# Weight loads on ScalarE's queue, and the last sums an eighth later, in a local-attention and whitening kernel

## The chip, the cores and the metric

The kernel runs on one core of a Trainium2 chip. A core has a matrix engine (TensorE, PE in the profile), a vector engine (VectorE, DVE), a scalar engine (ScalarE, ACT), a general engine (GpSimd, POOL) and SyncE (SP), which here only issues transfers. Each has its own queue of instructions and takes them in order; they meet through semaphores. PEld is the loading of weights into the matrix engine. The metric is device microseconds of one execution; the lower, the better.

## The reference

The input x has four images of 256 channels and 64 x 64 pixels, in float32.

```
k    = conv(x, w1, 7x7, dilation 2, pad 6) + b1      # 256 -> 128
k    = conv(k, w2, 1x1) + b2                         # 128 -> 49
attn = softmax(k, axis=1)                            # 49 taps for each pixel
xp   = pad(x, 6)
x    = sum over u, v of attn[7u + v] * xp[.., 2u:2u+64, 2v:2v+64]

# whitening, for each of four groups of 64 channels, over all images and pixels
xc    = x - mean;  Sigma = 1e-5 * I + xc @ xc.T / m
Sn    = Sigma / trace(Sigma);  P = I
5 times:  P = 1.5 * P - 0.5 * P^3 @ Sn
out   = (P / sqrt(trace(Sigma))) @ xc * weight + bias
```

So each image needs a convolution before its weighted sum, and the whitening matrix needs the sums of all four images before any output can be written.

## The kernel before

The two convolutions are one, with 49 outputs (w2 times w1). It is evaluated in seven points for each axis: the input of each of seven row points (`conv_step`) is combined on VectorE (`xh`, `ct`), multiplied on TensorE, and interpolated back on VectorE (`pv`, `zz`, at last `lgx`, the logits). A row point has three banks of column points, with one set of weights (`wr`) each. For the first image the transformed weights are made on the chip and written to DRAM (`gd`); for the later images `weights` loads them again (L419: 42 loads of about half a megabyte, in one buffer for each bank number). `conv_bank` does the matmuls of a bank (L599) into one of two PSUM buffers, `cv_buf`, and ScalarE copies them out (`pv`, L610 and L615).

The weighted sum of an image is cut into four units, n = 4b to 4b + 3, by parity of rows and columns, and each unit into `first_half` and `second_half`. `softmax(b, pc)` prepares two units: TensorE transposes the logits (L990), VectorE takes their maximum (L996), ScalarE the exponential, VectorE normalises and shuffles (L1034). `move_terms(n)` copies the terms into `zt` (L1075 on ScalarE; for the last image L1087 on VectorE), GpSimd writes them to DRAM (`sd`, L1092, eight transfers), and `load_band` reads them back skewed, as band matrices (L1127 and L1138, on SyncE). `make_block` transposes the pixels (L1168) and copies them to `xb` and `xbz` (L1174, L1182); `weighted_sum` multiplies them with the bands (L1210); `store_y` brings the result to SBUF (L1228, L1230); `turn_y` transposes it again (L1241, copied by ScalarE at L1249), and `moments` adds to mean and covariance (L1262). Transposes share three PSUM buffers, which `tp()` hands out. `make_block` and half of `store_y` use VectorE instead of ScalarE once `tail` is set. After odd units `move` may write a finished part of an image to DRAM (`spill`, L1280, 2 MB on GpSimd) and load other pixels in its place.

Two things set the order. The first is an order written by hand: the loop over images 1 to 3 takes the convolution's steps with costs of 6, 5 and 2, and each time an eighth of an image's cost is done, `gap(b, j)` runs what `plan` has put down for that eighth: the softmax of the image before, then its eight half-units. What is planned beyond the last eighth of image 3 runs after the convolution, with `tail` set. The second is the planner of the kernel language, which within this gives every engine its order by data and priorities. `softmax(b, 0)` and the copies under `high_priority` go first. `whiten` and the loop that applies it and writes the output follow, when all units are summed.

For the last two images the half-units stand at eighths 3 to 10 of the next image, in the kernel before: for image 3 all of them, and for image 2 the last three, lie after the convolution.

Of the kernel before, what the change touches and what calls it, by code (L numbers as in the profile page):

```python
# [32 lines left out]
def kernel(  # L33
# [29 lines left out]
    nc = tc.nc  # L63
    B, C, H, W = x.shape
# [30 lines left out]
    def taps(b):  # L95
        return (0,) if b == INF else (0, 1)
# [12 lines left out]
    def tp():  # L109
        return ps_tp.tile([P, 512], F32, tag="tp", name="tp")  # L110
# [72 lines left out]
    t = tp()  # L183
# [3 lines left out]
    t = tp()  # L187
# [4 lines left out]
    cv_buf = []  # L192
    for k in range(2):
        t = ps_cv.tile([P, 512], F32, name=f"cv{k}")
# [53 lines left out]
    for k, c0 in enumerate(range(0, P, CB)):  # L248
        n = min(CB, P - c0)
        t = cv_buf[k % 2]  # L250
# [15 lines left out]
    for k0 in range(0, KT, TB):  # L266
        n = min(TB, KT - k0)
        t = tp()
# [44 lines left out]
    for b in ORDER:  # L313
        slot_of[b] = nsl
        nsl += len(taps(b))
    gd = [
        dram.tile([P, nsl, NSK * len(taps(b)) // 2], F32, name=f"gd{b}") for b in range(NP)
    ]
# [27 lines left out]
    def add(o, a, b):  # L346
        return in_turn(TT(o, a, b, ALU.add))  # L347
# [57 lines left out]
    def weights(b, br, i, mid=None):  # L405

        first = (br, i) not in made
        made.add((br, i))
        s0 = slot_of[BANKS[i][0]]
        ns = sum(len(taps(bc)) for bc in BANKS[i])
        nk = NSK * len(taps(br)) // 2
        wt = apool.tile([P, ns, NSK], F32, tag=f"wr{i}", name=f"wr_{b}_{br}_{i}")[:, :, :nk]
        w = {bc: wt[:, slot_of[bc] - s0 : slot_of[bc] - s0 + len(taps(bc))] for bc in BANKS[i]}
        if not first:
            nc.sync.dma_start(wt, gd[br][:, s0 : s0 + ns])  # L419
            return w  # L420

        if br in kept:


            f = lgx if br == 4 else rb[0].rearrange("p q r c w -> p (q r c w)")
            f = f[:, : KS * nk]
            if i == 0:
                nc.sync.dma_start(f, kept[br])
            f = f.rearrange("p (v a r k) -> p v a r k", v=KS, a=NCC, k=KT)
            g = [f[:, v] for v in range(KS)]  # L430
        else:
            g = [gbr[:, v] for v in range(KS)]
        g = [t.rearrange("p a r k -> p (a r k)") for t in g]

        e = ct.rearrange("p a b -> p (a b)") if b else store[4].rearrange("p c r w -> p (c r w)")
        e, o, e1 = (e[:, k * nk : (k + 1) * nk] for k in range(3))
        g0 = [g[KS - 1 - a] for a in range(4)]
        g1 = [g[KS - 5 - a] for a in range(3)]
        o0 = {bc: w[bc][:, 0] for bc in w}
        o1 = {bc: w[bc][:, 1] for bc in w if bc != INF}  # L440

        def same(o, a):
            if br in kept:
                v = KS - 1 - a
                nc.sync.dma_start(o, kept[br][:, v * nk : (v + 1) * nk])
            else:
                nc.scalar.copy(o, g[KS - 1 - a])

        if i == 0:
            add(e, g0[0], g0[2])  # L450
            add(o, g0[1], g0[3])
            add(e1, g1[0], g1[2])
            add(o0[1], e, o)
            sub(o0[2], e, o)
            add(o1[1], e1, g1[1])
            sub(o1[2], e1, g1[1])
            same(o0[0], 0)
            same(o1[0], 4)
        elif i == 1:
            madd(e, g0[2], 4.0, g0[0])  # L460
            madd(o, g0[3], 4.0, g0[1])
            madd(e1, g1[2], 4.0, g1[0])
            madd(o0[3], o, 2.0, e)
            madd(o0[4], o, -2.0, e)
            madd(o1[3], g1[1], 2.0, e1)
            madd(o1[4], g1[1], -2.0, e1)
            same(o0[INF], 3)
        else:
            madd(o0[5], g0[0], 2.0, g0[1])
            madd(o1[5], g1[0], 4.0, g1[2])  # L470
            madd(o0[5], o0[5], 2.0, g0[2])
            if mid is not None:
                mid()
            madd(o1[5], g1[1], 2.0, o1[5])
            madd(o0[5], o0[5], 2.0, g0[3])
            add(o1[5], o1[5], o1[5])
        for bc in BANKS[i]:
            f = SCALE[bc] * (SCALE[br] if br not in kept else 1.0)
            if f != 1.0:
                nc.scalar.mul(w[bc], w[bc], f)  # L480
        nc.sync.dma_start(gd[br][:, s0 : s0 + ns], wt)
        return w
# [384 lines left out]
    for i in three:  # L867
        nxt.update(weights(0, 1, i))
# [94 lines left out]
    NI = NCH // 2  # L963
# [16 lines left out]
    def softmax(b, pc):  # L980

        lv = logits[b].rearrange("p r w -> p (r w)")
        nm = f"{b}_{pc}"
        mx = work.tile([P, NCH, 2], F32, tag="mx", name=f"mx_{nm}")
        lt = []
        for hf in range(2):
            lt.append(tp().rearrange("p (i h k) -> p i h k", i=NI, h=2))
            for i in range(NI):
                pe(
                    nc.tensor.transpose(  # L990
                        lt[hf][:, i].rearrange("p h k -> p (h k)")[:, :K2],
                        lv[:K2, bass.ds(2 * (NI * hf + i) * P + pc, P, 2)],
                        ident[:K2, :K2],
                    )
                )
            nc.vector.tensor_reduce(  # L996
                mx[:, NI * hf : NI * (hf + 1)], lt[hf][:, :, :, :KT], AX.X, ALU.max
            )
        nc.vector.tensor_scalar(mx, mx, -1.0, None, ALU.mult)  # L999
        d = terms[b, pc] = bpool.tile([P, 2, NCH, KT], F32, tag="d", name=f"d_{nm}", bufs=2)  # L1000
        s = work.tile([P, 2, NCH], F32, tag="s", name=f"s_{nm}")
        if b == B - 1:
            for hf in range(2):
                half = slice(NI * hf, NI * (hf + 1))
                nc.vector.tensor_tensor(
                    d.rearrange("p h i k -> p i h k")[:, half],
                    lt[hf][:, :, :, :KT],
                    mx[:, half].unsqueeze(3).to_broadcast([P, NI, 2, KT]),
                    ALU.add,
                )  # L1010
            for h in range(2):
                nc.scalar.activation(d[:, h], d[:, h], AF.Exp)
                nc.vector.tensor_reduce(s[:, h], d[:, h], AX.X, ALU.add)
        for h in range(2):
            for i in range(NCH) if b < B - 1 else ():
                nc.scalar.activation(  # L1016
                    d[:, h, i], lt[i // NI][:, i % NI, h, :KT], AF.Exp,
                    bias=mx[:, i, h : h + 1], accum_out=s[:, h, i : i + 1],
                )
            nc.vector.reciprocal(s[:, h], s[:, h])  # L1020
            rm = work.tile([P, NCH, KS], F32, tag="rm", name=f"rm_{nm}_{h}")
            nc.vector.tensor_tensor(
                rm,
                s[:, h].unsqueeze(2).to_broadcast([P, NCH, KS]),
                cmask.unsqueeze(1).to_broadcast([P, NCH, KS]),
                ALU.mult,
            )
            dh = d[:, h].rearrange("p i (u v) -> p i u v", u=KS)
            nc.vector.tensor_tensor(
                dh, dh, rm.unsqueeze(2).to_broadcast([P, NCH, KS, KS]), ALU.mult  # L1030
            )
        dv = d.rearrange("p h i (u v) -> p (h i u) v", u=KS)
        for step, vs in ((1, slice(4, 7, 2)), (2, slice(5, 7)), (-1, slice(0, 3, 2)), (-2, slice(0, 2))):
            last = nc.vector.stream_shuffle(  # L1034
                dv[:, :, vs], dv[:, :, vs], [(c - step) % SW for c in range(SW)]
            )

        return last
# [112 lines left out]
    tail = []  # L1151
# [177 lines left out]
    def bands(n, after=None):  # L1329

        move_terms(n, after)
        if n - 1 in half_done:
            load_band(n, 0)
        if n - 1 in done:
            load_band(n, 1)
            move_terms(n + 1, after)
# [26 lines left out]
    def plan(b, j, *what):  # L1363
        todo.setdefault((b + j // NPC, j % NPC), []).extend(what)

    def soft(b, pc):
        with tc.high_priority() if pc == 0 else nullcontext():
            last = softmax(b, pc)
        soft_done.add((b, pc))
        if pc == 0 and b == 0:  # L1370
            bands(0)

    for b in range(B):
        hs = [
            (lambda n=n, f=f: f(n))
            for n in range(4 * b, 4 * b + 4)
            for f in (first_half, second_half)
        ]
        if b + 2 < B:
            for j in range(8):  # L1380
                plan(b + 1, 2 + j, hs[j])
                if j == 3:

                    plan(b + 1, 2 + j, finish)
        else:
            for j in range(8):
                plan(b + 1, 3 + j, hs[j])
    for b in range(B):
        for j in range(2) if b else ():
            plan(b + 1, j, lambda b=b, j=j: soft(b, j))  # L1390
# [6 lines left out]
    for b in range(1, B):  # L1397
# [13 lines left out]
        j, at, whole = 0, 0, sum(c for c, _ in steps)  # L1411
# [242 lines left out]
```

## Time and profile before

| what | value |
|---|---|
| median of three runs (lowest, highest) | 739.77 us (734.72, 740.28) |
| the profiled execution | 736.93 us, its span 735.2 us |
| granted TensorE clock, mean | 0.974 |
| busy: TensorE, its weight loads | 687.0 us, 541.8 us |
| busy: VectorE, ScalarE, GpSimd | 594.5 us, 332.6 us, 133.2 us |
| convolution's matmuls (L599) | 234.1 us, 4160 of 275 ns |
| weighted sums (L1210) | 113.0 us, 512 of 347 ns |
| weight loads (L419) | 42, issued from 91.0 to 544.4 us, 0.33 us each to issue |
| GpSimd's writes of terms (L1092) | 128 of 533 ns |

A group's line in the profile names the line of code, the engine, the operation, output and input by the program's names, the shapes and the count; then busy time in us and the mean ns of one; then the idle time of the engine just before these instructions, and what ended most of it. In a list of waits a line has the waiting engine and line, what it waited for, the total in us, the number of times and the longest. A line of the timeline has its start, its length, and the same names. Times count from the span's start.

### The profile page before, as it was taken

The page shows a single profiled execution, that of the slowest core. Times are in us where ns is not written, and L with a number is a line of the kernel's source. Part 1 is how long each engine was busy: PE and PEld are TensorE (multiplying, and loading weights), DVE is VectorE, ACT ScalarE, POOL GpSimd, SP SyncE. Part 2 cuts the span into 40 slices and gives each one's busy share as a digit, 9 for nine tenths or more (in the row PEclk, how much of TensorE's full clock was granted, in tenths as well). Part 3 has the DMA queues.
Part 4 walks back from the last instruction along what each step waited for, and adds up shares of the span by engine and source line. Part 5 has one row for each costly group of instructions (what it writes and reads, how often), then busy time and mean ns, then how long its engine had stood idle before and what let it go on. Part 6 is the DMA issues. An engine that isn't in the chain of part 4 may idle for free.

```text
span 735.2 us, 19094 instructions
## 1 busy us (share of the span) xinstructions
PE 687.0 (93%) x7728; PEld 541.8 (74%) x7728; DVE 594.5 (81%) x1280; ACT 332.6 (45%) x930; POOL 133.2 (18%) x194
## 2 busy tenths in 40 slices
PE   6999999999898999988999999899999969997996
PEld 1449543478898988877999989898998858885231
DVE  3799998995796899989886899799959796435575
ACT  1424320133655654655555446727546422232564
POOL 0002526664031020020220200202202024200000
PEclk9999999999999999999999999999999978997899
DMA  8923999984665592147755820353623145463587
GB/s 321 260 91 105 238 364 234 224 184 91 174 170 146 209 292 68 62 131 252 214 128 187 279 69 11 98 163 76 182 83 79 45 89 130 107 249 140 235 362 319
DMA packets 78336, 126.09 MB, mean 172 GB/s; under 512 B 36471, under 2 KB 58664, under 8 KB 77096
## 3 DMA queue, kind: packets, MB, share of 16 engines
q1 hardware_dynamic: 65960, 82.79, 35.2%
q0 software_dynamic: 12288, 42.08, 22.1%
q8 instruction: 61, 1.00, 0.6%
q14 instruction: 27, 0.22, 0.1%
HBM read 78.78 MB, written 52.36 MB: 178 GB/s over the span
## 4 chain that ended last, share of the span: by engine, by line
PE 37%; DVE 26%; issue 9%; ACT 9%; POOL 4%; DMA 4%; SPq 0%; POOLq 0%; ACTq 0%; DVEq 0%
PE cv L599 16%; PE y L1210 6%; PE tp L1594 4%; DVE xh L354 3%; PE sig L1262 3%; DVE pv L354 3%; POOL ahead L147 3%; PE tp L1241 3%; DVE zz L354 2%; DMA band<-sd 2%; PE tp L1168 2%; DVE rb L347 2%; DVE rb L354 1%; ACT zt L1075 1%; POOL sd L1092 1%
## 5 line engine op out<-in xcount | busy, mean ns | idle before, releaser
L599 PE MATMUL cv<-xh,wr 128*49 128x128 f32 x4160 | 234.1, 275 | 0.0
L599 PEld LDWEIGHTS cv<-xh,wr 128*49 128x49 f32 x4160 | 229.1, 125 | 3.2 <-issue 1.3
L1092 POOL DMA_DIRECT2D sd<-zt x128 | 67.3, 533 | 310.5 <-ACT zt L1075 238.4
L1210 PE MATMUL y<-band,xb 128*128 128x209 f32 x512 | 113.0, 347 | 10.3 <-DMA band<-sd 10.1
L1210 PEld LDWEIGHTS y<-band,xb 128*128 128x128 f32 x512 | 87.5, 195 | 12.1 <-DMA band<-sd 9.1
L610 ACT COPY pv<-cv 113x486 f32<-113x486 f32 (+2 forms) x60 | 25.9, 432 | 98.4 <-PE cv L599 98.2
L1249 ACT COPY yt<-tp 128x256 f32<-128x256 f32 x128 | 45.5, 377 | 50.8 <-PE tp L1241 49.8
L1241 PE MATMUL tp<-ident,slot 128*128 128x128 f32 x256 | 52.4, 301 | 4.6 <-ACT yt L1249 3.0
L354 DVE SCALAR_TENSOR_TENSOR pv<-pv 113x162 f32<-113x162 f32 x176 | 52.9, 321 | 2.4 <-ACT pv L610 1.7
L1230 ACT ACTIVATE slot<-y,pivot 128x512 f32<-128x512 f32 x53 | 36.6, 739 | 35.6 <-PE y L1210 35.6
L1168 PE MATMUL tp<-ident,slot 128*128 128x128 f32 x256 | 50.2, 300 | 2.1 <-ACT xbz L1182 1.1
L1241 PEld LDWEIGHTS tp<-ident,slot 128*128 128x128 f32 x256 | 41.3, 205 | 12.5 <-ACT yt L1249 4.4
L1168 PEld LDWEIGHTS tp<-ident,slot 128*128 128x128 f32 x256 | 40.9, 204 | 5.9 <-ACT xbz L1182 1.4
L147 POOL DMA_DIRECT2D slot<-in_x_dram x20 | 33.9, 1695 | 51.4 <-issue 47.4
L1075 ACT COPY zt<-d 32x112 f32<-32x112 f32 (+2 forms) x132 | 38.2, 290 | 10.6 <-DVE d L1034 4.7
L354 DVE SCALAR_TENSOR_TENSOR xh<-ct 128x512 f32<-128x512 f32 x40 | 26.7, 689 | 18.5 <-PE cv L599 18.4
L1262 PE MATMUL sig<-yt 128*64 128x65 f32 x1024 | 37.5, 225 | 1.9 <-ACT yt L1249 1.9
L1262 PEld LDWEIGHTS sig<-yt 128*64 128x64 f32 x1024 | 32.8, 137 | 7.9 <-issue 4.1
L1016 ACT ACTIVATE d<-tp,mx 128x49 f32<-128x49 f32 x96 | 27.5, 332 | 19.2 <-DVE mx L999 19.2
L764 PE MATMUL acc<-slot,tap 128*49 128x256 f32 (+7 forms) x224 | 34.7, 468 | 0.0
L1174 ACT COPY xb<-tp 128x256 f32<-128x256 f32 x88 | 30.7, 377 | 8.1 <-PE tp L1168 7.8
L1228 DVE TENSOR_SCALAR slot<-y,pivot 128x512 f32<-128x512 f32 x11 | 8.3, 751 | 26.6 <-ACT slot L1230 26.6
(236 smaller groups left out, 1114.1 us busy)
## 6 DMA issues: line engine op xcount, KB each, us to landing
out_dram<-out SPq DMA_DIRECT2D x32, 512.0 KB, 3.6
band<-sd SPq DMA_DIRECT2D x64, 242.0 KB, 3.4
slot<-in_x_dram POOLq DMA_DIRECT2D x20, 512.0 KB, 7.3
sd<-zt POOLq DMA_DIRECT2D x128, 77.0 KB, 2.9
wr<-gd SPq DMA_DIRECT2D x14, 588.0 KB, 4.0
wr<-gd SPq DMA_DIRECT2D x14, 490.0 KB, 4.4
ahead<-in_x_dram POOLq DMA_DIRECT2D x12, 512.0 KB, 7.5
spill<-slot POOLq DMA_DIRECT2D x3, 2048.0 KB, 7.2
```

The costliest lines, as they stand in the source:

```text
L147: queue.dma_start(o[:, cc, h], src[:, :, pr, h * SW : (h + 1) * SW])
L354: return in_turn(STT(o, a, f, b, ALU.mult, ALU.add))
L599: nc.tensor.matmul(o, wv[:, sc, sr, cc], xv[bc][:, h * NCC + cc], start=(j == 0), stop=(j == len(terms) - 1), skip_group_check=True,)
L764: nc.tensor.matmul(ps[h * HB : h * HB + KT, :, o0:o1], w[v][:, cc], rhs, start=(j == 0 and k == 0), stop=(j == len(order) - 1), skip_group ...
L1075: ins = nc.scalar.copy(o, i)
L1092: nc.gpsimd.dma_start(bass.AP(tensor=D.tensor, offset=D.offset + h * HS + g * RS, ap=[[LS, TC], [CR * RS, NCH], [1, KS * WS]],), zt[p0 : p ...
L1168: nc.tensor.transpose(t[:, cc * P : (cc + 1) * P], tile_of(xt, cc, t8, h, pc), ident)
L1210: nc.tensor.matmul(ps[:, cc, q0 : q0 + nq, c0:c1], xb[:, cc * P : (cc + 1) * P], rhs, start=(k == 0), stop=(k == len(PIECES[half]) - 1), s ...
L1230: last = nc.scalar.activation(o, i, AF.Identity, bias=pivot[:, cc : cc + 1])
L1241: nc.tensor.transpose(t[:, cc * P : (cc + 1) * P], tile_of(yt, cc, i // 2, i % 2, pc), ident,)
L1249: return nc.scalar.copy(yb.rearrange("p a g c -> p (a g) c")[:, :, :GW], t[:, :C].rearrange("p (e c) -> p e c", c=GW),)
L1262: nc.tensor.matmul(sig[g * GW : (g + 1) * GW, cc], yb[:, cc, g, :GW], yb[:, cc, g], start=(count[0] == 0 and cc == 0), stop=(count[0] == 4 ...
```

## The change

Four edits, all in the stretch where convolution and sums run side by side, or at its end.

The weight loads of L419 are issued by ScalarE instead of SyncE. In ScalarE's order each stands just behind the copy out of the bank whose weights it replaces. The eight half-units of image 2 and of image 3 are planned one eighth later, so that one more half-unit comes after the convolution. The softmax of the last image transposes its logits into the two PSUM buffers of the convolution, which is done by then, instead of the three transpose buffers. And once the convolution is done, the terms of unit 12 are moved right after the first softmax of the last image.

```
@@ weights @@
         if not first:
-            nc.sync.dma_start(wt, gd[br][:, s0 : s0 + ns])
+            nc.scalar.dma_start(wt, gd[br][:, s0 : s0 + ns])
             return w
@@ softmax @@
         for hf in range(2):
-            lt.append(tp().rearrange("p (i h k) -> p i h k", i=NI, h=2))
+            t = cv_buf[hf] if b == B - 1 else tp()
+            lt.append(t.rearrange("p (i h k) -> p i h k", i=NI, h=2))
             for i in range(NI):
@@ soft @@
         soft_done.add((b, pc))
-        if pc == 0 and b == 0:
-            bands(0)
+        if pc == 0 and (b == 0 or tail):
+            bands(4 * b)
@@ the plan @@
         else:
             for j in range(8):
-                plan(b + 1, 3 + j, hs[j])
+                plan(b + 1, 4 + j, hs[j])
```

What else the edits move, in the order of the instructions of each engine: unit 10's first half comes after the convolution, so its eight block copies and one store go from ScalarE to VectorE (`tail`), where they stand behind the last interpolation. The first copy of unit 11 stands behind both softmaxes of the last image on VectorE. On GpSimd a spill of 2 MB now stands ahead of the writes of unit 4's terms, and the clearing of tiles for the whitening (L1423 to L1455) ahead of the writes of unit 11's. In the middle, TensorE's order for images 0 and 1 is the same.

## The prediction

> **What bounds the kernel now.** First the page's table of engines and its groups of instructions.
>
> ```profile
> PE 687.0 (93%) x7728; PEld 541.8 (74%) x7728; DVE 594.5 (81%) x1280; ACT 332.6 (45%) x930; POOL 133.2 (18%) x194
> ...
> L599 PE MATMUL cv<-xh,wr 128*49 128x128 f32 x4160 | 234.1, 275 | 0.0
> ...
> L1210 PE MATMUL y<-band,xb 128*128 128x209 f32 x512 | 113.0, 347 | 10.3 <-DMA band<-sd 10.1
> ...
> wr<-gd SPq DMA_DIRECT2D x14, 588.0 KB, 4.0
> wr<-gd SPq DMA_DIRECT2D x14, 490.0 KB, 4.4
> ```
>
> TensorE is busy for 687.0 of 735.2 us and the change removes none of its work, so everything at stake is TensorE's 48 us of idleness and its clock. The convolution's matmuls (L599) lost nothing; the weighted sums (L1210) lost 10.3 us, nearly all on band matrices. Next the waits of SyncE's queue, which issues both the bands and the weights (source, what it waited for, total us, times, longest):
>
> ```profile
> SPq L419 <- PE cv L599: 181.1, 35, 27.0
> ...
> SPq L1127 <- DMA sd<-zt: 42.7, 11, 20.8
> SPq L1127 <- PE y L1210: 27.1, 16, 4.9
> ```
>
> The weight loads stand at the head of this queue for 181.1 us, until the convolution frees their buffer, and each band load behind them stands too. What that costs TensorE is in its own waits, from 150 to 600 us, all from the middle of the kernel:
>
> ```profile
> PE y L1210 <- ACT xbz L1182: 5.7, 10, 1.5
> PE y L1210 <- DMA band<-sd: 4.3, 2, 2.5
> PE tp L990 <- ACT xb L1174: 3.5, 2, 1.9
> PE tp L1241 <- ACT yt L1249: 3.0, 6, 0.8
> ```
>
> Only two band waits, 4.3 us: nearly all of what stands in SyncE's queue delays nobody. Last, the stages (stretch, length, busy time of PE, PEld, DVE, ACT, POOL with counts, granted clock, DMA share, GB/s), and VectorE's stretch that decides the end of them:
>
> ```profile
> 530.00:562.00 32.00, 31.82 (x465) 30.18 (x461) 23.63 (x52) 16.56 (x47) 3.28 (x7) 1.00 0.36 92
> 562.00:580.00 18.00, 15.56 (x150) 14.18 (x150) 14.26 (x36) 11.39 (x28) 2.05 (x9) 1.00 0.34 80
> 580.00:600.00 20.00, 15.66 (x145) 13.53 (x144) 18.86 (x58) 6.60 (x15) 4.23 (x8) 0.96 0.18 30
> 600.00:615.00 15.00, 10.77 (x67) 9.00 (x68) 12.39 (x40) 1.48 (x3) 8.40 (x16) 0.60 0.74 168
> 615.00:663.00 48.00, 46.58 (x465) 42.57 (x465) 21.25 (x54) 15.55 (x35) 4.19 (x8) 1.00 0.54 167
> ```
>
> ```profile
> 540.01 0.69 DVE L354 SCALAR_TENSOR_TENSOR xh<-ct 128x512 f32<-128x512 f32 x1 [6.16 <-PE cv L599]
> ...
> 572.21 0.69 DVE L354 SCALAR_TENSOR_TENSOR lgx<-zz 113x512 f32<-113x512 f32 x1
> ...
> 592.46 2.49 DVE L1087 COPY zt<-d 128x56 f32<-128x56 f32 x11
> ...
> 608.43 0.42 DVE L1174 COPY xb<-tp 128x256 f32<-128x256 f32 x1
> ```
>
> The convolution ends at 561.9, VectorE finishes the last logits at 572.8 (call this T), then come the last softmax, its terms (zt, 592.5), their way through DRAM and the band of unit 12. TensorE runs out of other sums and idles 5.2 us before 602.9; the clock falls to 0.60 for 15 us; and unit 12 waits again for VectorE's copy at 608.4. Unit 12's first half ends at 613.5. From 615 on PE is 97% busy at full clock, so what happens before 613.5 is passed on to the end.
>
> [...]
>
> **The change part by part**, against the profiled execution (736.93 us: span 735.2 and 1.7 around it), which lies 2.8 under the median of 739.77.
>
> *Weight loads to ScalarE.* Relief: at most the 4.3 us of the two middle band waits. One of them, at unit 0, comes while the sums have barely begun; the other (2.50 us at 343.6, unit 4) follows four weight loads that held SyncE from 311.4 to 335.1. But GpSimd's order changes as well: unit 4's terms now stand behind the 2 MB spill of L1280, so its bands may come little earlier than the 339.6 of before. I take a gain of 1.5, bounds 0 and 4.3. Cost: 42 issues x 0.332 us = 13.9 us on ScalarE, which is 214.8 of 395 us busy between 150 and 545. TensorE's waits for ScalarE there sum to 16 us; with 13.9/214.8 = 6.5% more in that queue I let them grow by 1.0, and add 0.5 for VectorE waiting on pv evictions (L610) that stand behind an issue: 1.5, an estimate. Bounds: zero, if the issues fall into ScalarE's idle 180 us; 13.9, if none does. Each load stands after the eviction of the very bank whose weights it replaces, so its buffer is free when it comes; its landing of some 4 us has a whole evaluation of three banks before use. If a load did wait, the yt, xb and pv copies behind it would, and TensorE behind those. I take zero, the upper bound being in the 13.9.
>
> *Sums an eighth later.* The work is the same, in another place. Image 2's sums start two banks later, with later bands to spare: nothing by itself. At the end, unit 9's second half (6.3 us on TensorE) moves behind the last convolution bank, so the convolution ends at about 555.6. VectorE had waited 6.16 + 1.05 + 0.64 = 7.85 us for it; I let T come 6.3 earlier: 566.5. TensorE then has one half-unit more for the gap. Yet with the tail begun, unit 10's block copies (eight of 0.42 us) and one store (0.75) go from ScalarE to VectorE, 4.1 us, and they stand in its queue behind T. TensorE reaches them at about 563 and stands until 567. On GpSimd, the clearing of the whitening's tiles (L1423 to L1455, which ran at 573.0, with T, and takes 1.0) moves ahead of unit 11's eight writes, which began at 558.6 before: now 568 to 572.3, landing 2.9, band 3.4, so 578.6; TensorE wants it at about 581. Hidden by 2 us; late by the excess if T comes no earlier.
>
> *Softmax into the convolution's banks* (L987). Waits for the three transpose buffers around it (0.5, 0.5 and 0.4 us at 579.6, 589.5, 595.8) go; the value is inside the next sum.
>
> *Bands of unit 12 straight after the first last softmax* (L1370). Its 11 zt copies come earlier, but now the second softmax, too, stands ahead of unit 11's first copy (xb) on VectorE; before, unit 11's copies were interleaved with the first softmax (581.1 to 585.3). Working down VectorE's queue with the durations of before: copies of unit 10 to 570.4; store, two xb (tp at 572.9) to 573.7; the maxima (1.1), difference (0.2 + 1.0), sums (0.3 + 0.9), reciprocal, mask and product (1.5) to 578.8; store 579.6; two xb (after unit 10's moments) 581.0; four shuffles 583.8; maximum and 11 zt 586.8; second softmax to its first product 590.6; unit 11's xb at 591.0, its last xbz, with three shuffles (2.2) between, at 596.7. TensorE was ready for them at about 583: some 8 us of new wait. Then: unit 11's first half ends at 599 (yt, moments), second half + 6.3 = 605.5, unit 12's first half + 7.9 = 613.4. Its band (zt 586.8, eight issues of 0.53 to 591, landing 2.9, load 3.4) is there at 598, hidden. So 613.4 against 613.5; the clock, low after that wait, adds about 1.
>
> **Sum:** -1.5 + 1.5 + 1 = +1, 738 on the profiled basis and 740.8 on the median's; the runs of before scatter by 5.6 us, and I write 740.
>
> **Rivals.**
> 1. *The gap is filled* (about 731). From T to unit 12's copies VectorE took 35.6 us, of which 3.7 idle. Kept busy it needs 31.9 + 4.1 = 36.0: 566.5 + 36 = 602.5, unit 12 ending 4 to 5 us later (5.1 before, at the low clock): 6 to 7 less. TensorE's own sums from 566 on would end at 604. With T the full 7.85 earlier another 1.5 goes: about 8.5 in all. For: 5.2 us of idleness and 6 us lost at the clock of 0.60 are there to be had. Against: the queue's order above.
> 2. *The new wait costs more than the old one* (748, the slower side). Its place is unit 11's xb behind the second softmax. A gap of 8 us is longer than the 5.2 that brought 0.60 for 15 us; trickling copies keep it there until 605, and TensorE's 14 us of unit 11 take up to 8 us more. It decides as soon as TensorE waits there over 5 us and the clock doesn't return before unit 11's second half. For: the order. Against: copies and shuffles may run ahead when T comes the full 7.85 earlier.
> 3. *SyncE's freedom is worth little and ScalarE's issues show* (747): the loads fall at bank ends, where yt and xb copies are due, and half of the 13.9 us is exposed.
> 4. *The change doesn't do what it says*: bands wait for sd (42.7 us) or for y (27.1) instead of for weights; then the gain of 1.5 is nought. It lies within the forecast.
>
> **How the numbers follow.** Forecast (733 to 746) 0.45; rival 1 0.22; rival 2 0.22; rival 3 0.11. A measurement of this kernel can hardly tell less than 1% (7.4 us) from no change. Rival 1 lies below 732.4 for the most part: faster 0.22. Rivals 2 and 3: slower 0.33. Same 0.45. The range of 8 in 10 reaches from 729 to 752.
>
> **What would show it.** SyncE's queue has no L419 and its waits are for sd and y alone; ScalarE is some 14 us busier in its queue; the logits' last interpolation ends at 565 to 567; the first zt copies of unit 12 lie at 584 to 587; TensorE waits 6 to 9 us for VectorE's xb in unit 11, with a clock under 0.8 after it, and no longer for a band at unit 12. I am wrong if that wait is under 3 us (then about 731), or if TensorE's waits for yt and xb grow by over 5 us in the middle.

## The result, and the profile after

The changed kernel takes 739.14 us (median of 20 runs, 735.80 to 741.55), the kernel before, run beside it, 737.52 us (20 runs, 734.61 to 741.45). The ratio is 1.002, with a 95% interval of 1.0004 to 1.0036: 0.2% slower, so nothing that matters. 740 had been forecast, and "no change" as the likeliest case. The profiled execution has a span of 734.0 us, 1.2 under that of before: by one execution alone the change would have looked like a small gain.

From line 987 on, the lines of the changed kernel are one higher than before (L1210 is L1211). The page:

```profile
PE 684.0 (93%) x7728; PEld 539.1 (73%) x7728; DVE 598.0 (81%) x1291; ACT 328.8 (45%) x919; POOL 133.2 (18%) x194
...
L599 PE MATMUL cv<-xh,wr 128*49 128x128 f32 x4160 | 231.5, 273 | 3.5 <-ACT xh L547 3.3 <-DMA wr<-gd 0.2
...
L1211 PE MATMUL y<-band,xb 128*128 128x209 f32 x512 | 113.4, 348 | 7.0 <-DMA band<-sd 5.9
...
wr<-gd ACTq DMA_DIRECT2D x14, 588.0 KB, 5.3
wr<-gd ACTq DMA_DIRECT2D x14, 490.0 KB, 4.3
```

TensorE's work is the same. The convolution's matmuls, which had never waited, now lose 3.5 us; the weighted sums lose 5.9 us on bands instead of 10.1. The waits of SyncE's queue, which no longer issues weights:

```profile
SPq L1128 <- DMA sd<-zt: 211.9, 19, 45.9
...
SPq L1139 <- PE y L1211: 40.7, 11, 12.2
SPq L1128 <- PE y L1211: 38.6, 20, 6.0
```

The 181.1 us that weight loads had stood at the head of this queue are gone, and in their place its band loads wait for the terms themselves (`sd`). The queue is free earlier, but what it has to load isn't there yet. TensorE's waits in the middle, from 150 to 560 us:

```profile
PE y L1211 <- ACT xbz L1183: 5.5, 8, 1.5
PE y L1211 <- DMA band<-sd: 5.1, 3, 2.0
PE cv L599 <- ACT xh L547: 3.3, 1, 3.3
PE tp L991 <- ACT xb L1175: 2.0, 2, 1.3
```

Over the same stretch the bands cost 4.3 us before. At unit 4 they cost 1.28 + 2.05 us, where they had cost 2.50: its terms now stand behind the spill, and GpSimd is done with them at 330.1 instead of 327.3. The waits for ScalarE sum to 13.4 us (13.2 before), in other places.

Then the end, by stages (columns as in the prediction):

```profile
562.00:580.00 18.00, 17.41 (x166) 16.09 (x166) 15.09 (x41) 9.30 (x26) 5.32 (x15) 1.00 0.44 94
580.00:600.00 20.00, 11.62 (x73) 9.50 (x72) 18.20 (x59) 3.05 (x7) 4.88 (x10) 0.66 0.23 46
600.00:615.00 15.00, 13.64 (x136) 12.26 (x135) 9.45 (x29) 4.45 (x10) 7.73 (x15) 1.00 0.68 155
```

The hole has moved from 600-615 (clock 0.60) to 580-600 (clock 0.66), one stage earlier. Its price at the clock is the same: it is at half (0.50) for 13.7 us each time, from 598.4 to 612.1 before and from 584.2 to 597.8 now. VectorE's timeline there:

```profile
562.93 0.69 DVE L354 SCALAR_TENSOR_TENSOR lgx<-zz 113x512 f32<-113x512 f32 x1
...
580.80 2.48 DVE L1088 COPY zt<-d 128x56 f32<-128x56 f32 x11
...
584.12 1.04 DVE L1006 TENSOR_TENSOR d<-cv,mx 128x392 f32<-128x392 f32 x2
...
587.67 0.42 DVE L1175 COPY xb<-tp 128x256 f32<-128x256 f32 x1
...
591.45 0.42 DVE L1175 COPY xb<-tp 128x256 f32<-128x256 f32 x1
```

In this profile the last logits come 9.3 us earlier (562.9 instead of 572.2), the terms of unit 12 11.7 us earlier (580.8 instead of 592.5). But the block copies of unit 11's first half stand behind the second softmax, from 587.7 on. (Its first two blocks are made at the end of unit 10, and were copied at 576.8.) ScalarE and TensorE around it:

```profile
585.19 0.95 ACT L1013 ACTIVATE d<-d 128x392 f32<-128x392 f32 x2 [6.27 <-DVE d L1006]
586.05 0.35 ACT L1250 COPY yt<-tp 128x256 f32<-128x256 f32 x1
```

```profile
586.45 0.70 PE L1242 MATMUL tp<-ident,slot 128*128 128x128 f32 x2 [5.91 <-ACT yt L1250]
588.58 0.70 PE L1169 MATMUL tp<-ident,slot 128*128 128x128 f32 x2 [1.42 <-DVE xbz L1183]
...
591.93 1.76 PE L1211 MATMUL y<-band,xb 128*128 128x209 f32 x4 [0.83 <-DVE xb L1175]
```

ScalarE stands 6.27 us in front of the exponentials of the second softmax, for which VectorE's differences come at 584.1. The copy of yt that frees TensorE's transpose buffer is queued behind them. TensorE waits 5.91 + 1.42 + 0.83 = 8.2 us, and works at the low clock (0.50) until 597.8. The band of unit 12, the wait of 5.2 us before, now costs 0.9. Here are that wait and the last products of unit 12's first half, before:

```profile
602.93 1.76 PE L1210 MATMUL y<-band,xb 128*128 128x209 f32 x4 [5.15 <-DMA band<-sd]
...
612.85 0.69 PE L1210 MATMUL y<-bandz,xbz 128*128 128x96 f32 x4
613.46 1.15 PE L1262 MATMUL sig<-yt 128*64 128x65 f32 x32
```

and after:

```profile
607.02 0.98 PE L1211 MATMUL y<-band,xb 128*128 128x209 f32 x4 [0.89 <-DMA band<-sd]
...
610.76 0.69 PE L1211 MATMUL y<-bandz,xbz 128*128 128x96 f32 x4 [0.41 <-DVE xbz L1183]
611.38 1.15 PE L1263 MATMUL sig<-yt 128*64 128x65 f32 x32
```

The weighted sums of unit 12's first half end at 611.4, against the 613.5 of before; counted to the end of the moments behind them, as in the experiments below, it is 612.5 against 614.6. Two executions of one order differ by more than these 2 us (e5 below).

### The profile page after: what moved, and what is told of

Same layout as the page of the kernel before. It is cut to its first block, busy times and chain, and to the rows that moved or that the text cites. A ratio compares the mean times of both kernels' runs of the same rounds, so it can differ in the third digit from the quotient of the medians.

```text
span 734.0 us, 19103 instructions
## 1 busy us (share of the span) xinstructions
PE 684.0 (93%) x7728; PEld 539.1 (73%) x7728; DVE 598.0 (81%) x1291; ACT 328.8 (45%) x919; POOL 133.2 (18%) x194
## 4 chain that ended last, share of the span: by engine, by line
PE 38%; DVE 27%; issue 9%; ACT 6%; DMA 4%; POOL 4%; ACTq 0%; SPq 0%; POOLq 0%; DVEq 0%
PE cv L599 15%; PE y L1211 7%; PE tp L1595 4%; DVE xh L354 3%; PE tp L1242 3%; DMA band<-sd 3%; DVE pv L354 3%; POOL ahead L147 3%; PE sig L1263 3%; DVE zz L354 2%; PE tp L1169 2%; DVE rb L347 2%; DVE rb L354 2%; ACT d L1017 1%; DVE pv L350 1%
## 5 line engine op out<-in xcount | busy, mean ns | idle before, releaser
L599 PE MATMUL cv<-xh,wr 128*49 128x128 f32 x4160 | 231.5, 273 | 3.5 <-ACT xh L547 3.3
L599 PEld LDWEIGHTS cv<-xh,wr 128*49 128x49 f32 x4160 | 226.3, 124 | 6.9 <-ACT xh L547 3.5
L1211 PE MATMUL y<-band,xb 128*128 128x209 f32 x512 | 113.4, 348 | 7.0 <-DMA band<-sd 5.9
L1211 PEld LDWEIGHTS y<-band,xb 128*128 128x128 f32 x512 | 87.8, 195 | 8.9 <-DMA band<-sd 4.8
L1175 ACT COPY xb<-tp 128x256 f32<-128x256 f32 x82 | 28.5, 376 | 11.6 <-PE tp L1169 11.1
```

The lines of the kernel that those rows point to most:

```text
L599: nc.tensor.matmul(o, wv[:, sc, sr, cc], xv[bc][:, h * NCC + cc], start=(j == 0), stop=(j == len(terms) - 1), skip_group_check=True,)
L1211: nc.tensor.matmul(ps[:, cc, q0 : q0 + nq, c0:c1], xb[:, cc * P : (cc + 1) * P], rhs, start=(k == 0), stop=(k == len(PIECES[half]) - 1), s ...
```

## The experiments

Each run is compared with the kernel before on the same chip. The medians are of 20 to 22 runs, for e1 and e11 of 14, for e9 of 13, for e12 of 12 and for e7 of 6. The edits are counted as in the text on the change: loads, postponed sums, banks, unit 12's terms. Together:

| run | what | median us | ratio to before | 95% interval |
|---|---|---|---|---|
| the change | | 739.14 | 1.0020 | 1.0004 to 1.0036 |
| e1 | before, loads on ScalarE | 738.70 | 0.9997 | 0.9974 to 1.0020 |
| e2 | change, loads back on SyncE | 737.43 | 0.9981 | 0.9968 to 0.9995 |
| e3 | change, sums not postponed | 739.06 | 1.0017 | 0.9999 to 1.0035 |
| e4 | change, second softmax late | 736.46 | 0.9974 | 0.9959 to 0.9990 |
| e5 | change without the fourth edit | 739.70 | 1.0028 | 1.0012 to 1.0044 |
| e6 | e4 with loads on SyncE | 735.46 | 0.9975 | 0.9960 to 0.9989 |
| e7 | e6 with block copies on ScalarE | 729.81 | 0.9906 | 0.9878 to 0.9933 |
| e8 | change with block copies on ScalarE | 734.50 | 0.9960 | 0.9946 to 0.9975 |
| e9 | e7 with loads on ScalarE | 732.27 | 0.9912 | 0.9883 to 0.9941 |
| e10 | change, logits in transpose buffers | 739.61 | 1.0025 | 1.0007 to 1.0043 |
| e11 | change, each load cut in two | 737.14 | 0.9995 | 0.9971 to 1.0019 |
| e12 | e7, sums not postponed | 732.32 | 0.9925 | 0.9896 to 0.9954 |

The theory (M in what was expected) was that the loads move for nothing and that the new wait in unit 11 eats what the earlier logits bring. Its rival (R, the third of the prediction) was that the loads on ScalarE cost what the rest gains.

### The weight loads alone, and taken back

e1 is the kernel before with the first edit alone, e2 the changed kernel without it.

```
-            nc.sync.dma_start(wt, gd[br][:, s0 : s0 + ns])
+            nc.scalar.dma_start(wt, gd[br][:, s0 : s0 + ns])
```

> The kernel before with the first edit alone: the 42 later weight loads issued by ScalarE. Theory M (the loads move at no cost and no gain; the end of the kernel decides the change): within 2 us of before, ratio 0.997 to 1.003; TensorE's wait for unit 4's band (2.5 us) goes or halves, and ScalarE's 14 us of issues are hidden. Theory R (the loads cost what the other edits gain): 3 to 5 us slower, ratio 1.004 to 1.007, with longer waits of TensorE for yt, xb and xbz of ScalarE in the middle.

> The changed kernel with the loads back on SyncE: sums an eighth later, last logits in the convolution's banks, unit 12's terms early. Theory M: as the changed kernel, ratio to before 1.000 to 1.004, with the same wait of 8 us in unit 11's first half. Theory R: 3 us faster than before, ratio 0.996.

On the kernel before, the loads make no difference that 14 runs can tell (0.9997). The 2.5 us of unit 4's band didn't go: in e1's profile TensorE waits 6.4 us for bands in the middle, 4.3 before:

```profile
PE y L1210 <- DMA band<-sd: 6.4, 3, 3.4
```

e2, 0.9981, lies below what M had and above what R had. Its tail is that of the change to a tenth: 5.9 us for yt, 1.4 and 0.8 for VectorE's copies. So the wait in unit 11 has nothing to do with the loads. Whether the loads cost something beside the postponed sums, 0.4% by this pair, is tested again below, with two other pairs and by cutting each load in two.

### The sums at their old place

e3 is the changed kernel with one line of the plan as before.

```
-                plan(b + 1, 4 + j, hs[j])
+                plan(b + 1, 3 + j, hs[j])
```

> The changed kernel with the sums of images 2 and 3 at eighths 3 to 10 again, the other edits kept. Theory M: the last logits' interpolation ends at about 571 to 573 again, unit 11's copies stand among those of the first softmax and the 8 us wait in unit 11 is gone, the wait for unit 12's band of 5 us is back; the time is that of before less up to 2 us (loads, and the waits for the transpose buffers), ratio 0.997 to 1.000. Theory R: 3 to 5 us slower than before.

The last logits' interpolation starts at 574.0 instead of 562.9. The wait for yt in unit 11 is gone, and the wait for unit 12's band is back, in TensorE's timeline of e3:

```profile
604.50 1.76 PE L1211 MATMUL y<-band,xb 128*128 128x209 f32 x4 [5.94 <-DMA band<-sd]
...
607.51 1.76 PE L1211 MATMUL y<-band,xb 128*128 128x209 f32 x4 [0.39 <-DMA band<-sd]
```

The time, 1.0017, isn't told apart from that of the change (1.0020), nor from before. That it would be up to 2 us under before was wrong. One hole takes the place of the other at about the same price (in e3 a wait of 5.9 us and a clock of 0.68 from 600 to 615, in the change 8.2 us and 0.66 from 580 to 600), and it is the second edit, the postponed sums, that exchanges them.

### The second softmax after unit 11's first half

In e4 the second softmax of the last image is planned one eighth later than in the changed kernel.

```
-            plan(b + 1, j, lambda b=b, j=j: soft(b, j))
+            plan(b + 1, 2 * j if b == B - 1 else j, lambda b=b, j=j: soft(b, j))
```

> The changed kernel with the second softmax of the last image planned after unit 11's first half instead of before it. Theory M: the waits of 5.9, 1.4 and 0.8 us in unit 11's first half go, it ends at about 586, unit 11 at 592; unit 12's band is there at 594 to 595, so 2 us of wait come back; unit 12's first half ends at 603 to 605 instead of 612.5, and the time falls by 6 to 8 us, ratio to before 0.990 to 0.993. Rival B: the second softmax is then late for unit 13, whose band makes TensorE wait 6 us or more: the gain shrinks to 0 to 2 us, ratio 0.998 to 1.002.

0.9974, a gain of some 0.5% on the change, half of what was expected. The wait for yt is gone, and no band is late (0.7 us), so rival B isn't it either. TensorE's waits of e4 after 550 us:

```profile
PE tp L1169 <- DVE xbz L1183: 5.4, 2, 3.8
PE y L1211 <- DVE xbz L1183: 2.2, 4, 1.0
PE y L1211 <- DVE xb L1175: 1.2, 1, 1.2
```

8.8 us for VectorE's block copies: VectorE, busy for 17.4 of the 20 us from 580 to 600, is itself short of time. The working had treated VectorE's order as the trouble; its load, with the copies that `tail` gives it, is a second one, which e7 and e8 test.

### The fourth edit undone

```
-        if pc == 0 and (b == 0 or tail):
-            bands(4 * b)
+        if pc == 0 and b == 0:
+            bands(0)
```

> The changed kernel without its fourth edit (unit 12's terms right after the first softmax of the last image). The order of the instructions on every engine is then that of the changed kernel, instruction for instruction, since the terms of unit 12 were planned in the same place anyway. Expected: the changed kernel's time, ratio to before 1.000 to 1.004; it also tells how far two measurements of one program lie apart.

1.0028, the changed kernel's time, as it must be: the two programs have the same instructions in the same order on all five engines, so the fourth edit does nothing. Its profile shows how far two executions of one order differ. The last logits' interpolation starts at 566.4 in one and at 562.9 in the other, and the clock from 500 to 530 is 0.95 in one and 1.00 in the other, from 330 to 360 0.89 and 0.94. A difference of 3 us between two single profiles says nothing here.

### Loads on SyncE and the late softmax together

> The changed kernel with the weight loads back on SyncE and the second softmax after unit 11's first half. If the loads on ScalarE cost 1.7 us or more beside the postponed sums, as the two earlier runs suggest, the gains add up: ratio to before 0.993 to 0.996. If that difference was scatter: 0.996 to 0.999.

0.9975, as with the loads on ScalarE (e4, 0.9974): the gains of e2 and e4 don't add up.

### The block copies back on ScalarE

e7 adds one line in two places to e6, and e8 the same to the changed kernel.

```
-            (nc.vector.tensor_copy if tail else nc.scalar.copy)(xb, t[:, :C])
+            (nc.vector.tensor_copy if n > 12 else nc.scalar.copy)(xb, t[:, :C])
```

> As the run before it, and the block copies (xb, xbz) of units 10 to 12 stay on ScalarE, 24 copies of some 0.4 us less on VectorE between the last logits and unit 12. Theory M (VectorE's queue bounds the stretch from the last logits to unit 12): TensorE's waits for VectorE's xb and xbz, 8.8 us with the second softmax late, go; 2 us of waits for the bands of units 12 and 13 each come instead; unit 12's first half ends at 599 to 602, and the time is 6 to 10 us under before, ratio 0.986 to 0.992. Rival B (the way through DRAM of units 12 and 13 is the bound): the band waits are 4 us or more each, ratio 0.993 to 0.997.

> The changed kernel with the block copies of units 10 to 12 on ScalarE, nothing else. Theory M: VectorE's second softmax comes 4 us earlier, but ScalarE's copy of yt still stands behind the exponentials of that softmax (5.9 us of wait in the changed kernel, here 3 to 6), while the waits for VectorE's xb go: 2 to 4 us under the changed kernel, ratio to before 0.996 to 0.999. Were VectorE's queue alone to blame and ScalarE's not, the whole wait of 8 us would go: ratio 0.990.

e7 takes 729.81 us, 0.9906: it beats both kernels. The stages of its end, and TensorE's waits after 550 us:

```profile
562.00:580.00 18.00, 16.21 (x167) 14.51 (x161) 11.25 (x27) 14.31 (x40) 5.33 (x15) 1.00 0.32 69
580.00:600.00 20.00, 17.68 (x163) 16.29 (x163) 15.49 (x47) 11.09 (x31) 4.19 (x8) 1.00 0.57 131
600.00:615.00 15.00, 13.21 (x132) 11.68 (x130) 8.92 (x35) 7.09 (x19) 8.40 (x16) 1.00 0.65 153
...
PE y L1211 <- DMA band<-sd: 3.7, 3, 1.7
...
PE y L1211 <- DVE xbz L1183: 0.8, 2, 0.4
```

The clock is full in all three. VectorE has 34 copies fewer, 13.9 us (the 24 in the expectation was a miscount); it is busy for 15.5 of the 20 us in which it had 18.2, ScalarE for 11.1 instead of 3.1. TensorE's waits for VectorE's copies are down to 0.8 us, and three waits for bands came in their place: 2.0 us at unit 11 and 1.7 at unit 13 (units 12 and 13 had been expected). Unit 12's first half ends at 604.3 (expected 599 to 602).

e8, 0.9960, is what M had. In unit 11, 3.6 us of wait are left, for ScalarE's xb and xbz, and 1.7 for its band. ScalarE stands 5.68 us before the same exponentials, and the block copies are now queued behind them with yt:

```profile
589.54 0.95 ACT L1013 ACTIVATE d<-d 128x392 f32<-128x392 f32 x2 [5.68 <-DVE d L1006]
590.39 0.35 ACT L1175 COPY xb<-tp 128x256 f32<-128x256 f32 x1
```

So both queues had made the wait of 8 us. Against the change, e4 gains 0.5%, e8 0.6%, and both edits together (e9 below) 1.1%: the two shares add up.

### The loads once more

> The fastest kernel so far (second softmax late, block copies of units 10 to 12 on ScalarE), with the weight loads on ScalarE as in the change. If the loads there cost some 3 us beside the postponed sums (as the changed kernel against the one with the loads back on SyncE would say): ratio to before 0.994 to 0.996. If they cost nothing (as the two kernels with the late softmax would say): 0.989 to 0.992.

e11 cuts each load in two, which gives 84 issues in its trace, of 0.33 us each (the middle number, in ns):

```profile
L420 ACTq DMA_DIRECT2D wr<-gd x84: 325/327/1569, 92.3 to 538.7; - x84
```

```
-            nc.scalar.dma_start(wt, gd[br][:, s0 : s0 + ns])
+            for u, v in ((0, ns // 2), (ns // 2, ns)):
+                nc.scalar.dma_start(wt[:, u:v], gd[br][:, s0 + u : s0 + v])
```

> The changed kernel with each of the 42 weight loads cut in two transfers of half the size on ScalarE's queue: up to 84 issues of 0.33 us, the same bytes. If the issuing time on ScalarE is what the loads cost, 1.5 to 3 us come on top, ratio to before 1.004 to 1.007, and the waits of TensorE for ScalarE grow in the middle. If the issues are hidden: no change from the changed kernel, 1.001 to 1.004.

e9 against e7 is 0.9912 against 0.9906, no difference that these runs can tell. e11, with the issuing time doubled, is not slower than the change (0.9995 against 1.0020; the intervals overlap). ScalarE's issues are hidden, as far as these intervals tell. Of four pairs with and without the loads on ScalarE, three show no difference, and the fourth (the change and e2) 0.4%. What that 0.4% is stays open; that it isn't the issuing time is shown by e11.

One difference in the middle can be seen. With the loads on ScalarE the planner orders two of ScalarE's copies the other way round, and with the sums postponed TensorE waits 3.3 to 3.7 us once for the later of them (xh, L547, at 497). With the loads on SyncE it is 1.5 us for pv. In both, ScalarE had stood (6.5 us in the change, 4.8 us in e2) before a copy (L541) that waits for VectorE, with the eviction of a finished bank behind it. In the kernel before, ScalarE stood there for 4.6 us as well, but TensorE had sums to do from 496.4 on, and no such wait. The 0.4% isn't explained by it: e4 and e6 differ in the same two waits (3.7 and 1.5 us) and not in time.

### The banks for the last logits

```
-            t = cv_buf[hf] if b == B - 1 else tp()
-            lt.append(t.rearrange("p (i h k) -> p i h k", i=NI, h=2))
+            lt.append(tp().rearrange("p (i h k) -> p i h k", i=NI, h=2))
```

> The changed kernel with the last softmax's logits in the three transpose buffers again. The second softmax's transposes then hold two of the three buffers until VectorE has taken the maxima and differences, and unit 11's transposes stand behind them. Theory M: unit 11 stands behind VectorE's second softmax anyway, so only the waits of 0.4 to 0.5 us for a buffer come back: 0 to 2 us slower than the changed kernel, ratio to before 1.002 to 1.005. If the banks were what made the early second softmax possible at all: 4 us or more, ratio over 1.007.

1.0025. The wait in unit 11 is nearly as long (7.3 us) and has another name, in TensorE's waits of e10 after 550 us:

```profile
PE tp L1241 <- DVE d L1005: 4.4, 1, 4.4
PE y L1210 <- DVE xb L1174: 2.9, 1, 2.9
```

Now it is the transpose buffer that VectorE's second softmax holds. The banks do what they are for, but the same softmax is waited for at the next place.

### The postponed sums under the better tail

e12 is e7 with the plan of before (the edit of e3).

> The fastest kernel so far (loads on SyncE, second softmax after unit 11's first half, block copies of units 10 to 12 on ScalarE) with the sums of images 2 and 3 at eighths 3 to 10 again, as before the change. Theory M (the postponed sums are worth some 7 us as soon as VectorE's queue lets TensorE do them): the last logits come at 572 to 574 again, TensorE is done with unit 11 before unit 12's band comes, and a wait of 4 us or more for that band is back; 4 to 7 us slower than with the sums postponed, ratio to before 0.996 to 1.000. If the late softmax and the copies alone bring the gain: 0.989 to 0.993.

0.9925: only 1 to 1.5 us slower than with the sums postponed (0.9906 and 0.9912), and the intervals overlap. M had 4 to 7 us there, and falls in this point. The mechanism is seen: the last logits come 5.3 us later (571.0 against 565.7), TensorE waits 5.0 us for unit 12's band, and unit 12's first half ends at 609.5 instead of 604.3. The wait, in e12's timeline:

```profile
598.47 1.76 PE L1211 MATMUL y<-band,xb 128*128 128x209 f32 x4 [5.01 <-DMA band<-sd]
```

But of these 5.2 us only 2.6 are left when the output loop begins (674.5 against 671.9): e7 waits another 1.7 us for a later band at 615, which e12 doesn't. So most of the gain on the kernel before comes from the late softmax and the moved copies, not from the place of the sums; which of these two counts for how much with the sums at their old place wasn't tried. In the kernel before, too, the copies of unit 11 lay between the logits and the terms of unit 12: 592.5 - 572.2 = 20.3 us, in e12 588.2 - 571.0 = 17.2.

## Why the prediction was right

The time was right, 740 against 739.14, and the mechanism was the one forecast: a gain at the end of the convolution, spent again in unit 11. Not every step was. That 740 lies within 1 us is in part luck: the 739.77 that it started from was the median of three runs, over 2 us above that of twenty, and the two terms for the loads, neither of which was there, cancelled in the sum. What makes the 1.6 us (0.2%) between the medians isn't shown: the hole costs about as much as before, and the pair of the change and e2 puts 0.4% on the loads beside the postponed sums, for a reason that stays open.

- *Loads to ScalarE.* Forecast: a gain of 1.5 and a cost of 1.5. Measured alone: nothing (e1), which the sum of the two gives as well; it is the waits that show neither term was there. The band waits in the middle rose from 4.3 to 5.1 us, since SyncE's queue now waits for the terms, and unit 4's terms for the spill, as feared. The waits for ScalarE went from 13.2 to 13.4 (up to 560 us; the 16 that the prediction put "between 150 and 545" are those up to 600). The fourth rival, that bands wait for `sd` instead, holds.
- *Sums an eighth later.* T was to come 6.3 us earlier, at 566.5; the two profiles of this order show the last interpolation ending at 563.6 and 567.1. VectorE did its part. Ten block copies went over to it, six xb and four xbz, where eight had been counted; yet the stand of some 4 us that was foreseen for TensorE before them came to 0.3. That postponing image 2's sums is "nothing by itself" was wrong in the small: 3.3 us of wait (1.5 with the loads on SyncE) in a convolution with fewer sums between its banks. GpSimd's clearing ahead of unit 11's writes was hidden, as said: the writes began at 566.6.
- *Bands of unit 12 straight after the first softmax of the last image.* The step that failed. It laid the second softmax ahead of unit 11's copies to the fourth edit. That edit moves nothing (e5); the second edit does it, since with the sums postponed unit 11 is planned behind the second softmax (e3).
- *The 8 us of new wait.* The size was right, 8.2, and the clock after it (0.66). The name was not: unit 11's xb was to be late, and the first and longest part, 5.9 us, is ScalarE's yt, queued behind exponentials that wait for VectorE. The trace shows both engines keeping the order of their queues here. ScalarE stood 6.27 us before the exponentials, and yt, transposed by 579.6, was copied at 586.05, straight behind them. VectorE stood 0.60 us before the sums of the second softmax (L1014, at 585.75), and a block of unit 11, transposed by 580.6, was copied behind them, at 587.67. The prediction followed this order through VectorE's queue in unit 11, and through ScalarE's only for the weight loads.
- *The sum.* The weighted sums of unit 12's first half were to end at 613.4, where they had ended at 613.5. They did at 611.4 in this profile and at 615.0 in that of the same order in e5: the size was right, as far as single profiles tell. Its terms were copied by 583.3 (586.8 forecast; the first copies, looked for at 584 to 587, came at 580.8), and its band was 0.9 us late. That all of this "is passed on to the end" holds in part: of e12's 5.2 us, 2.6 were left at the output loop.
- *Rival 1*, the gap filled, about 731, is not what the change does. e7 does it, with 729.81 us.
- *Rival 2*, the new wait dearer than the old: it came over 5 us, but the clock was back at 1.00 from 597.8 on, as unit 11's second half began. Its point of decision was not reached.
- *Rival 3*, exposed issues: refuted by e11.

## What to carry to other kernels

Before work is moved into a hole, follow the queue of each engine that this work needs on its way there: here the sums reached the hole, and their helpers on VectorE and ScalarE stood behind a softmax that could have waited (e4). ScalarE, standing 6.27 us for VectorE, passed that wait on to the yt queued behind it, and TensorE's 5.91 us carry ScalarE's name: the engine named in a wait need not be the one to relieve. And an edit is judged by undoing it alone: of the four edits here one moved no instruction at all, and a queue that stood for 181 us was nobody's bottleneck.

## What the runs showed that was not expected

One order of instructions gave two profiles in which the last logits lie 3.5 us apart, with a lower clock in that of e5. In the changed kernel's profile TensorE stood 3.3 us before 497.4, and the clock from 500 to 530 was 1.00; in e5 it was 0.95, with TensorE busy for 16.5 us from 480 to 500 in both. From 330 to 360, where TensorE stood 1.28 and 2.05 us for unit 4's bands in the changed kernel's profile, the clock was 0.94 there and 0.89 in e5. The times of one program spread over 5.8 us (735.80 to 741.55), and they go with the clock: of the 20 runs of the change, the two with a mean clock of 0.977 took 735.8 us, the four with 0.968 took 740.6 to 741.6. It takes some twenty runs of each to see 0.2%.

Nor did the clock fall at the same length of a gap. In the kernel before, the clock fell to half at 598.4, only 0.6 us into the gap of 5.2 us before unit 12; from 595.0 to 598.3 TensorE had been busy for 2.1 of the 3.3 us. In the changed kernel it fell 3.7 us into its gap.
